# Layer norm of the next image in the selective scan's own PSUM pool, and the block's last copy in another place of ScalarE's queue

## The chip, the core and the metric

One core of one Trainium2 chip runs the whole program, a chain of four layers. The metric is the device time in microseconds, the median of several runs; less is better. One further execution was recorded by the hardware profiler, and all durations of single instructions come from it.

## The reference, cut to what matters

Two images of 128 channels and 64x64 pixels pass an attention layer, a convolution layer with deformed sampling, three steps of a residual convolution, and then the layer that is changed here, a selective scan in four directions:

```python
x_norm = _layernorm(x_flat, ln_w, ln_b)          # over the 128 channels of a pixel
def _mamba(x, ...):
    xh, z = jnp.split(x @ W_in.T, 2, axis=-1)
    xh = silu(causal_conv4(xh) + conv_b)
    dt, Bm, Cm = split(xh @ W_xp.T)
    dt = softplus(dt @ W_dt.T + b_dt)
    dA, dBu = exp(dt[..., None] * A), dt[..., None] * Bm[:, :, None, :] * xh[..., None]
    h_t = dA_t * h_{t-1} + dBu_t                 # 256 channels x 16 states, 4096 pixels
    y = einsum(h, Cm) + xh * Dp
    return (y * silu(z)) @ W_out.T
out = x + W_fuse @ concat(mamba of rows, rows reversed, columns, columns reversed) + b_fuse
```

## The kernel before, in words

The last layer is `layer3`. Each image and direction is cut into 8 **blocks** of 512 pixels, so there are 64 blocks, numbered i: image 0's four directions (rows; columns; columns reversed; rows reversed), then image 1's (columns; columns reversed; rows; rows reversed). A block has 8 **groups** k (two halves of 128 channels times four sets of four states), and each group four **scans** of 128 x 512 on VectorE. A group's place in its block, k mod 8, is called its slot. The order of all work is written by hand: within `tc.manual_schedule()` each engine's queue holds its instructions in the order in which the Python code issues them, and the framework adds the waits.

Four PSUM pools share the memory: `psd` (three tiles `da`, the decays), `psb` (two `pbc`), `psy` (one `py`) and `psm` (two `pm3`, for everything else).

One turn of the main loop, for group k in slot s of block i:

- `weights(k + 2)` on TensorE (L1370) spreads B over partitions into `pbc`.
- Four times: `expo` on ScalarE (L1402) makes the decay `da` of the scan that is two ahead; in the first of the four, `keep` (L1416) saves the last state of the group before; `scan` on VectorE (L1411). An expo needs a free `da`, so it waits for the scan that read that tile last. In two slots of a block `gate` (L1438) stands between the second and the third scan.
- `db_dve` (L1386, VectorE) and `db_pool` (L1395, GpSimd) make the inputs of the next group's scans, `cmul` (L1421, GpSimd) multiplies the scanned states by C.
- The front of the *next* block by slot: slot 0 `conv_silu` (ScalarE, L1289, L1290, with two loads of activation tables); 1 `xproj` and `xproj_copy`; 2 and 3 `delta` (TensorE, L1334) and `softplus` (ScalarE, four instructions, L1340 to L1343), one half each; 4 `xproj_rest` (L1326, L1327) and `rest_copy` (L1330); 5 `zproj` (L1296) and `zproj_silu` (L1302, L1303); 6 and 7 `conv` (L1284), one half each.
- The end of the *previous* block: in slot 3 `project` on TensorE (L1446 adds the old pixels by an identity matrix, L1448 twice the output weights) into a `pm3` tile; in slot 4, after everything else that ScalarE does there, `finish`, one copy out of that tile: L1454 in a first direction, L1456 in the second and third, L1459 in the last, to a tile named `sq` that is then stored.
- `sums(k - 2)` on TensorE (L1429) adds up a group over its states, which frees its `db` buffer, one of four.

Layer norm of image 0 runs ahead of the loop, in a prologue over `t`, in which the front of block 0 is spread too. Layer norm of image 1 is done during blocks 22 to 29, 512 pixels in each, by `next_norm`. Before the change its steps are: slot 6 `ln_mean` (TensorE, L1211, by a matrix of 1/128, into a `pm3` tile); slot 7 `ln_square` (VectorE subtracts the mean, L1222; ScalarE squares, L1223); and in the next block slot 0 `ln_var` (TensorE, L1227, another `pm3`); slot 1 `ln_scale` (ScalarE, L1231 Ln and L1232 Exp; GpSimd multiplies, L1233); slot 2 `ln_store` (ScalarE, L1242). It stands at the end of a turn, ahead of `sums`. Image 1's `sq` and `xc` are single buffers, and `sq` is shared with the result tile of L1459.

```python
                for q in range(4):
                    if 4 * k + q + AHEAD < len(units):
                        expo(*units[4 * k + q + AHEAD])
                    if q == 0 and ended:
                        keep(k - 1)
                    if live:
                        scan(k, q)
                ...
                front_pe(i + 1, slot)
                front_act(i + 1, slot)
                front_pool(i + 1, slot)
                if i >= 1 and i <= NBK:
                    if slot == 3:
                        project(i - 1)
                    elif slot == 4:
                        finish(i - 1)
```

Of the kernel before, what the change touches and what calls it, by code (L numbers as in the profile page):

```python
# [10 lines left out]
F32 = mybir.dt.float32  # L11
# [4 lines left out]
AF = mybir.ActivationFunctionType  # L16
# [4 lines left out]
P = 128  # L21
NB = 2
HW = 64
L = HW * HW
BLK = 512
NBLK = L // BLK
RB = BLK // HW
# [25 lines left out]
def interior(g, b, r0=0, rows=HW):  # L53
    return g.xa[:, b, 1 + r0 : 1 + r0 + rows, 1 : 1 + HW]
# [7 lines left out]
def img(t):  # L62
    return t.rearrange("p (r w) -> p r w", w=HW)
# [1057 lines left out]
def layer3(g, I, out):  # L1121
# [5 lines left out]
    nc, tc = g.nc, g.tc  # L1127
# [6 lines left out]
    with ExitStack() as ctx:  # L1134
# [71 lines left out]
        N = {}  # L1206


        def ln_mean(b, k):
            N[k, "mean"] = psm.tile([P, BLK], F32, name="pm3")  # L1210
            nc.tensor.matmul(N[k, "mean"], onesm, interior(g, b, k * RB, RB), start=True, stop=True)  # L1211

        def ln_square(b, k):
            if b == 0:

                t = wk.tile([P, 4, BLK], F32, name="db")
                N[k, "xc"], N[k, "sq"] = t[:, 0, :], t[:, 1, :]
            else:
                N[k, "xc"] = ck.tile([P, BLK], F32, name="xc", bufs=1)
                N[k, "sq"] = ck.tile([P, BLK], F32, name="sq", bufs=1)  # L1220
            xc = N[k, "xc"]
            nc.vector.tensor_sub(img(xc), interior(g, b, k * RB, RB), img(N[k, "mean"]))  # L1222
            nc.scalar.activation(N[k, "sq"], xc, AF.Square)  # L1223

        def ln_var(b, k):
            N[k, "var"] = psm.tile([P, BLK], F32, name="pm3")
            nc.tensor.matmul(N[k, "var"], onesm, N[k, "sq"], start=True, stop=True)  # L1227

        def ln_scale(b, k):

            nc.scalar.activation(N[k, "sq"], N[k, "var"], AF.Ln, bias=g.eps5)  # L1231
            nc.scalar.activation(N[k, "sq"], N[k, "sq"], AF.Exp, scale=-0.5)  # L1232
            nc.gpsimd.tensor_mul(N[k, "xc"], N[k, "xc"], N[k, "sq"])  # L1233

        def by_row(k):
# [214 lines left out]
        def finish(i):  # L1450
            b, nd, c = blocks[i]
            s_ = S.pop(i)
            if nd == 0:
                nc.scalar.activation(s_["xv"], img(s_["pf"]), AF.Identity, bias=vec(g, "b_fuse"))  # L1454
            elif nd < 3:
                nc.scalar.copy(s_["xv"], img(s_["pf"]))  # L1456
            else:
                res = ck.tile([P, BLK], F32, name="sq", bufs=1)
                nc.scalar.copy(res, s_["pf"])  # L1459
                nc.sync.dma_start(out[b, :, c * BLK : (c + 1) * BLK], res)  # L1460

# [62 lines left out]
                if slot in (3, 4):  # L1524
                    spread(i, slot - 3)

        LN = {6: ln_mean, 7: ln_square, 8: ln_var, 9: ln_scale, 10: ln_store}

        def next_norm(i, slot):

            for j, s in ((i, slot), (i - 1, slot + 8)):
                b, k = divmod(j, 4 * NBLK)
                k -= 4 * NBLK - 2 - NBLK
                if j >= 0 and b + 1 < NB and 0 <= k < NBLK and s in LN:
                    LN[s](b + 1, k)

        with tc.manual_schedule():
            tc.keep_in_program_order(nc.scalar.preload_act_table_set("natural_log_exp_and_others"))
            nc.scalar.activation(am, am, AF.Exp)
            nc.vector.tensor_scalar(am, am, -1.0, None, ALU.mult)  # L1540
            nc.vector.memset(xt[:, :HC], 0.0)
            nc.vector.memset(xt[:, HC + L :], 0.0)
            nc.vector.memset(xn[:, HB - 1, HW - HC :], 0.0)
            nc.vector.memset(xn[:, HB + HW, :HC], 0.0)

            for t in range(NBLK + 2):
                slot = t - 2
                if slot == 6:
                    for k in range(2):
                        weights(k)  # L1550
                    db_dve(0)
                    db_pool(0)
                if slot >= 0:
                    front_pe(0, slot)
                    front_act(0, slot)
                    front_pool(0, slot)
                if slot == 1:
                    bc_store(0)
                elif slot in (3, 4):
                    spread_store(0, slot - 3)  # L1560
                    if slot == 3:
                        spread_load(0, 0)
                        copies(0, "b", 0)
                        copies(0, "c", 0)
                for s in LN:
                    if 0 <= t - s // 8 < NBLK:
                        LN[s](0, t - s // 8)
                if t == 1:
                    begin(0)
                    conv(0, 1)  # L1570
            for ng in range(1, NNG):
                copies(0, "b", ng)
                copies(0, "c", ng)
            units = [(k, q) for k in range(len(groups)) for q in range(4)]
            AHEAD = 2
            for u in range(AHEAD):
                expo(*units[u])
            for k in range(len(groups) + 6):
                i, slot = divmod(k, 8)
                live = k < len(groups)  # L1580
                more = k + 1 < len(groups)
                ended = 1 <= k <= len(groups)
                transfers(i + 1, slot)
                if k + 2 < len(groups):
                    weights(k + 2)
                for q in range(4):
                    if 4 * k + q + AHEAD < len(units):
                        expo(*units[4 * k + q + AHEAD])
                    if q == 0 and ended:
                        keep(k - 1)  # L1590
                    if live:
                        scan(k, q)

                    for j, hf in (((k - 6) // 8, 0), ((k - 10) // 8, 1)):
                        if q == 1 and 8 * j + 6 + 4 * hf == k and 0 <= j < NBK:
                            gate(j, hf)
                if more:
                    db_dve(k + 1)
                    db_pool(k + 1)
                if ended:  # L1600
                    cmul(k - 1)
                front_pe(i + 1, slot)
                front_act(i + 1, slot)
                front_pool(i + 1, slot)
                if i >= 1 and i <= NBK:
                    if slot == 3:
                        project(i - 1)
                    elif slot == 4:
                        finish(i - 1)
                if live:  # L1610
                    next_norm(i, slot)

                    if slot == 6 and i % (4 * NBLK) < NBLK // 2:
                        for n in range(2):
                            turn(blocks[i][0], 2 * (i % (4 * NBLK)) + n)

                if 0 <= k - 2 < len(groups):
                    sums(k - 2)
# [159 lines left out]
```

## Time and profile before

| what | value |
|---|---|
| median of 3 runs | 5967.48 us (5966.78 to 5974.58) |
| the profiled execution: its own time | 5965.63 us |
| the profiled execution: span from first to last instruction | 5963.8 us |
| busy: TensorE, VectorE, ScalarE, GpSimd | 4905.1, 4521.3, 3768.4, 3653.1 us |
| first scan starts, last scan ends | 2517.65, 5948.17 us |
| granted TensorE clock, mean | 0.86 |

The span in 40 slices of 149 us; a digit is the busy share in tenths, PEclk the granted clock in tenths:

```profile
DVE  5333333364134688599999999999999999999998
ACT  4888888830035411477666766767776766767665
POOL 5111111100010121299999999999999999999998
PEclk8999999999989899877778777877788777877776
```

From slice 18 on it is the scan stage: VectorE and GpSimd are full, ScalarE is at two thirds, and TensorE's clock changes all the time. In the groups of instructions, a line gives the busy us, the mean ns of one, and the idle time of its engine just before, with what ended it. In a list of waits a line gives who waited, for whom, the us in total, how many times and the longest. A timeline line gives start, length, engine, line, operation, tiles (out<-in) and shape; equal neighbours are merged, and a bracket holds idle time before it and its releaser.

### The profile page before, as it was taken

To read this page: it belongs to the slowest core of one execution; us is meant where nothing else is said; L and a number is where in the kernel's file an instruction comes from. 1 tells how busy PE (TensorE), PEld (TensorE's weight loads), DVE (VectorE), ACT (ScalarE), POOL (GpSimd) and SP (SyncE) were. 2 spreads that over 40 slices of the span, in tenths; PEclk is the share of its full clock that TensorE was granted. 3 is DMA by queue.
4 is the path that set the end of the run, shared out by engine and by line. 5 is a ranking of instruction groups with operands and counts; after the bars stand their busy time and mean duration, and the time that the engine had idled before them with its cause. 6 is when DMAs were issued, how large, how long until landed. Compare 5 with 4: busy or idle time off the path is not lost.

```text
span 5963.8 us, 57478 instructions
## 1 busy us (share of the span) xinstructions
PE 4905.1 (82%) x18726; PEld 1661.7 (28%) x18726; DVE 4521.3 (76%) x4266; ACT 3768.4 (63%) x5371; POOL 3653.1 (61%) x1328
## 2 busy tenths in 40 slices
PE   7999999989978689877777777777777777777776
PEld 3333333334444234222222222222222222222221
DVE  5333333364134688599999999999999999999998
ACT  4888888830035411477666766767776766767665
POOL 5111111100010121299999999999999999999998
PEclk8999999999989899877778777877788777877776
DMA  5000001030066100255555555554565555555554
GB/s 153 18 18 18 19 18 33 1 58 1 15 116 113 48 4 0 52 135 123 125 126 139 135 123 124 128 134 116 136 139 131 127 122 130 139 130 126 126 136 99
DMA packets 333092, 541.85 MB, mean 91 GB/s; under 512 B 66504, under 2 KB 121168, under 8 KB 331696
## 3 DMA queue, kind: packets, MB, share of 16 engines
q1 hardware_dynamic: 329648, 534.54, 39.0%
q10 hardware_dynamic: 3136, 3.56, 0.2%
q8 instruction: 149, 2.44, 0.2%
q14 instruction: 159, 1.30, 0.1%
HBM read 448.78 MB, written 89.13 MB: 90 GB/s over the span
## 4 chain that ended last, share of the span: by engine, by line
PE 39%; DVE 37%; ACT 6%; issue 6%; DMA 6%; POOL 4%; SPq 1%; DVEq 0%; POOLq 0%; ACTq 0%
DVE db L1411 25%; PE ps L287 10%; DVE db L1386 10%; PE acc L303 8%; PE m L1052 5%; PE m L566 5%; DMA dx<-dd 3%; POOL db L1421 2%; ACT da L1402 2%; PE acd L812 2%; PE pm L1296 1%; PE m L526 1%; ACT L1303 1%; ACT L1302 1%; PE pf L775 1%
## 5 line engine op out<-in xcount | busy, mean ns | idle before, releaser
L1421 POOL TENSOR_TENSOR db<-db,c 128x2048 f32<-128x2048 f32 x512 | 2310.7, 4528 | 21.6 <-ACT hl L1416 21.1
L1411 DVE TENSOR_TENSOR_SCAN db<-da,hl,db 128x512 f32<-128x512 f32 x1792 | 2165.0, 1265 | 61.3 <-ACT da L1402 14.9
L1402 ACT ACTIVATE da<-dd,am 128x512 f32<-128x512 f32 x2048 | 1403.5, 689 | 963.3 <-DVE db L1411 953.7
L293 ACT ACTIVATE e<-ps 128x1024 f16<-128x1024 f32 x1024 | 992.2, 1021 | 134.7 <-PE ps L287 117.5
L1386 DVE TENSOR_TENSOR db<-pbc,dd 128x2048 f32<-128x2048 f32 (+2 forms) x512 | 851.8, 1664 | 19.8 <-PE py L1429 18.2
L1370 PE MATMUL pbc<-bc,sel 64*128 64x512 f32 x512 | 288.5, 564 | 571.7 <-DVE db L1386 571.4
L1395 POOL TENSOR_TENSOR db<-b,dd 128x1024 f32<-128x1024 f32 (+1 forms) x256 | 671.6, 2623 | 119.9 <-issue 94.5
L1429 PE MATMUL py<-db,fold 128*32 128x512 f32 x4096 | 640.5, 703 | 104.8 <-POOL db L1421 104.7
L314 DVE RECIPROCAL rec<-acc 32x512 f32<-32x512 f32 x64 | 214.9, 3358 | 639.2 <-PE acc L303 612.1
L321 POOL TENSOR_TENSOR parts<-parts 32x512 f32<-32x512 f32 x64 | 80.4, 1256 | 975.3 <-DVE parts L320 975.3
L287 PE MATMUL ps<-q,k 32*128 32x512 f32 x4096 | 656.2, 643 | 3.5 <-DVE flag L250 2.7
L303 PE MATMUL acc<-e,v 128*128 128x512 f16 x2048 | 531.3, 382 | 0.0
L1052 PE MATMUL m<-v,u 128*128 128x512 f32 x864 | 377.2, 600 | 51.0 <-DVE v L1021 51.0
L1370 PEld LDWEIGHTS pbc<-bc,sel 64*128 64x128 f32 x512 | 106.2, 208 | 1113.4 <-DVE db L1386 1048.3
L1284 PE MATMUL pm<-xn,wcs 128*128 128x512 f32 x512 | 285.0, 708 | 56.9 <-DVE xc L1222 46.3
L1411 DVE TENSOR_TENSOR_SCAN db<-da,db 128x512 f32<-128x512 f32 x256 | 294.4, 1205 | 17.4 <-ACT da L1402 8.7
L303 PEld LDWEIGHTS <-v 128*128 128x128 bf16 x2048 | 158.5, 97 | 509.8 <-issue 388.5
L287 PEld LDWEIGHTS ps<-q,k 32*128 32x128 f32 x4096 | 229.7, 183 | 227.9 <-issue 147.1
L1284 PE MATMUL pm<-xt,wcs 128*128 128x512 f32 x512 | 279.2, 696 | 11.3 <-ACT z L1302 11.3
L1427 PE MATMUL py<-u,ddp 128*128 128x512 f32 x256 | 186.4, 818 | 101.7 <-DVE gt L1438 101.7
L566 PE MATMUL m<-comb,w 64*128 64x512 f32 (+4 forms) x1296 | 269.9, 575 | 0.0
L686 POOL TENSOR_SCALAR yt<-y 32x512 f32<-32x512 f32 x8 | 18.2, 2270 | 381.2 <-DVE y L677 380.8
(315 smaller groups left out, 5970.5 us busy)
## 6 DMA issues: line engine op xcount, KB each, us to landing
dd<-dx SPq DMA_DIRECT2D x1024, 256.0 KB, 6.6
dx<-dd SPq DMA_DIRECT2D x128, 512.0 KB, 8.7
c<-bx SPq DMA_DIRECT2D x1024, 64.0 KB, 2.3
hats<-pos SPq DMA_DIRECT2D x136, 256.0 KB, 9.6
b<-bx SPq DMA_DIRECT2D x512, 64.0 KB, 5.2
q<-qd SPq DMA_DIRECT2D x32, 512.0 KB, 8.6
w<-in_conv0T SPq DMA_DIRECT2D x18, 288.0 KB, 8.5
q<-in_x SPq DMA_DIRECT2D x8, 512.0 KB, 7.6
```

The lines of the kernel that those rows point to most:

```text
L287: nc.tensor.matmul(ps[:, i, :], k4[h % 2][rows, kb // 4, :], q4[h % 2][rows, qb * BLK : (qb + 1) * BLK], start=True, stop=True,)
L293: nc.scalar.activation(e[:, :n, :], ps[:, :n, :], AF.Exp)
L303: nc.tensor.matmul(acc, v3[b][:, kb, h, :], e[:, i, :], start=(kb == 0), stop=(kb == NS - 1))
L566: yield lambda q=q, dy=dy, src=src, i0=i0, i1=i1: nc.tensor.matmul(m[:, i0 * NF : i1 * NF], w[half, dy, q, x, :], src, start=(dy == KC and ...
L1052: nc.tensor.matmul(m[x], weights[j][:, dy, x, :], v[j][b][:, x, r0 : r0 + RP, :].rearrange("p r i -> p (r i)"), start=(dy == 0), stop=(dy ...
L1284: nc.tensor.matmul(pu, wcs[:, hf, s, :], window(blk, sgn * s), start=(s == 0), stop=(s == 3))
L1386: nc.vector.tensor_tensor(x["db"][:, :n, :], x.pop("pb").unsqueeze(1).to_broadcast([P, n, BLK]), S[i]["d4", hf][:, 1, :n, :], ALU.mult)
L1395: nc.gpsimd.tensor_tensor(x["db"][:, n:, :], S[i]["b", ng].unsqueeze(1).to_broadcast([P, 4 - n, BLK]), S[i]["d4", hf][:, 1, n:, :], ALU.mult)
L1402: nc.scalar.activation(da, S[i]["d4", hf][:, 0, q, :], AF.Exp, scale=am[:, hf, q, ng : ng + 1])
L1411: nc.vector.tensor_tensor_scan(d1, d0, d1, 0.0 if first else hl[:, hf, ng, q, :], ALU.mult, ALU.add)
L1421: nc.gpsimd.tensor_mul(v, v, S[i]["c", ng].unsqueeze(1).to_broadcast([P, 4, BLK]))
L1429: nc.tensor.matmul(S[i]["y", hf][32 * q : 32 * q + 32, :], fold, G[k]["db"][:, q, :], start=False, stop=(ng == NNG - 1),)
```

## The change

It has four parts, all in `layer3`.

1. Mean and variance of layer norm are written to `da` tiles of `psd` instead of `pm3` tiles of `psm`, in the prologue and in the loop.
2. In the loop, the steps of image 1's layer norm stand in other slots, in the turn of the same block: slot 0 `ln_mean` (right after the first expo) and `ln_less` (the subtraction, after the scans); slot 1 `ln_square` (now the square alone, after `xproj_copy`); slot 3 `ln_var` (after the first expo), `ln_log` (before the last expo) and `ln_root` (after softplus); slot 4 `ln_scale` (GpSimd's multiplication alone); slot 6 `ln_store`. In the prologue their order stays.
3. `finish` is issued at the start of slot 4, ahead of the four expos, for every block.
4. The result tile of L1459 gets a name and so a buffer of its own; the loop has one more turn.

```diff
+        def ln_tile():
+            return psd.tile([P, BLK], F32, name="da")
+
         def ln_mean(b, k):
-            N[k, "mean"] = psm.tile([P, BLK], F32, name="pm3")
+            N[k, "mean"] = ln_tile()
             nc.tensor.matmul(N[k, "mean"], onesm, interior(g, b, k * RB, RB), start=True, stop=True)
 
-        def ln_square(b, k):
+        def ln_less(b, k):
...
-            xc = N[k, "xc"]
-            nc.vector.tensor_sub(img(xc), interior(g, b, k * RB, RB), img(N[k, "mean"]))
-            nc.scalar.activation(N[k, "sq"], xc, AF.Square)
+            nc.vector.tensor_sub(img(N[k, "xc"]), interior(g, b, k * RB, RB), img(N[k, "mean"]))
+
+        def ln_square(b, k):
+            nc.scalar.activation(N[k, "sq"], N[k, "xc"], AF.Square)
 
         def ln_var(b, k):
-            N[k, "var"] = psm.tile([P, BLK], F32, name="pm3")
+            N[k, "var"] = ln_tile()
             nc.tensor.matmul(N[k, "var"], onesm, N[k, "sq"], start=True, stop=True)
 
+        def ln_log(b, k):
+            nc.scalar.activation(N[k, "sq"], N[k, "var"], AF.Ln, bias=g.eps5)
+
+        def ln_root(b, k):
+            nc.scalar.activation(N[k, "sq"], N[k, "sq"], AF.Exp, scale=-0.5)
+
         def ln_scale(b, k):
-            nc.scalar.activation(N[k, "sq"], N[k, "var"], AF.Ln, bias=g.eps5)
-            nc.scalar.activation(N[k, "sq"], N[k, "sq"], AF.Exp, scale=-0.5)
             nc.gpsimd.tensor_mul(N[k, "xc"], N[k, "xc"], N[k, "sq"])
...
-                res = ck.tile([P, BLK], F32, name="sq", bufs=1)
+                res = ck.tile([P, BLK], F32, name="res", bufs=1)
...
-        LN = {6: ln_mean, 7: ln_square, 8: ln_var, 9: ln_scale, 10: ln_store}
-
-        def next_norm(i, slot):
-            for j, s in ((i, slot), (i - 1, slot + 8)):
-                b, k = divmod(j, 4 * NBLK)
-                k -= 4 * NBLK - 2 - NBLK
-                if j >= 0 and b + 1 < NB and 0 <= k < NBLK and s in LN:
-                    LN[s](b + 1, k)
+        def next_norm(i):
+            b, k = divmod(i, 4 * NBLK)
+            k -= 4 * NBLK - 2 - NBLK
+            return (b + 1, k) if b + 1 < NB and 0 <= k < NBLK else None
...
-                for s in LN:
-                    if 0 <= t - s // 8 < NBLK:
-                        LN[s](0, t - s // 8)
+                if t < NBLK:
+                    for part in (ln_mean, ln_less, ln_square):
+                        part(0, t)
+                if 0 <= t - 1 < NBLK:
+                    for part in (ln_var, ln_log, ln_root, ln_scale, ln_store):
+                        part(0, t - 1)
...
-            for k in range(len(groups) + 6):
+            for k in range(len(groups) + 7):
...
+                norm = next_norm(i)
+                if slot == 4 and 1 <= i <= NBK:
+                    finish(i - 1)
                 for q in range(4):
+                    if norm and slot == 3 and q == 3:
+                        ln_log(*norm)
                     if 4 * k + q + AHEAD < len(units):
                         expo(*units[4 * k + q + AHEAD])
+                    if norm and q == 0:
+                        if slot == 0:
+                            ln_mean(*norm)
+                        elif slot == 3:
+                            ln_var(*norm)
                     if q == 0 and ended:
                         keep(k - 1)
...
+                if norm and slot == 0:
+                    ln_less(*norm)
                 if more:
                     db_dve(k + 1)
                     db_pool(k + 1)
...
-                if i >= 1 and i <= NBK:
-                    if slot == 3:
-                        project(i - 1)
+                if slot == 3 and 1 <= i <= NBK:
+                    project(i - 1)
+                if norm:
+                    if slot == 1:
+                        ln_square(*norm)
+                    elif slot == 3:
+                        ln_root(*norm)
                     elif slot == 4:
-                        finish(i - 1)
+                        ln_scale(*norm)
+                    elif slot == 6:
+                        ln_store(*norm)
                 if live:
-                    next_norm(i, slot)
```

## The prediction, made before the run

> **What bounds the kernel now.** I read the page's costliest groups first. The scan stage (2517.6 to 5948.2 us in the trace, 58% of the span) belongs to VectorE; it waits 61 us in all before 1792 scans, and most of ScalarE's idle time is waiting for scans.
>
> ```profile
> L1411 DVE TENSOR_TENSOR_SCAN db<-da,hl,db 128x512 f32<-128x512 f32 x1792 | 2165.0, 1265 | 61.3 <-ACT da L1402 14.9
> L1402 ACT ACTIVATE da<-dd,am 128x512 f32<-128x512 f32 x2048 | 1403.5, 689 | 963.3 <-DVE db L1411 953.7
> ```
>
> Then busy time by stretch (columns: busy us of PE, PEld, DVE, ACT, POOL with counts, clock, DMA): before the blocks that also normalise image 1 (22 to 29), during them, after them.
>
> ```profile
> 2517.60:3688.50 1170.90, 886.02 (x2510) 246.41 (x2509) 1146.38 (x924) 822.04 (x1330) 1120.44 (x351) 0.80 0.56 130
> 3688.50:4190.70 502.20, 382.76 (x1068) 112.09 (x1068) 474.48 (x386) 353.79 (x572) 471.27 (x153) 0.79 0.54 127
> 4190.70:5948.20 1757.50, 1321.15 (x3752) 366.02 (x3752) 1720.39 (x1385) 1212.01 (x1965) 1687.82 (x524) 0.79 0.55 129
> ```
>
> VectorE is 98% busy outside and 94% inside the middle stretch. From first scan to first scan a block takes 53.49 us (51.73 for the last of a direction, since scans without an initial state are shorter); the nine blocks 22 to 30 take 502.3 instead of 9 x 53.49 - 1.75 + 8 x 0.60 = 484.5 us, where 0.60 is what the added subtraction takes of VectorE's queue. So about **17.8 us** can be won there. The waits of 3742 to 4191 us say where they lie:
>
> ```profile
> DVE db L1386 <- PE py L1429: 18.2, 8, 2.9
> PE pm L1284 <- DVE xc L1222: 46.3, 8, 6.2
> ```
>
> The mean sits in a `pm3` tile (two buffers) until VectorE's L1222, so conv's second half (L1284) waits for it on TensorE, the sums (L1429) queue behind it, and L1386 misses its db buffer.
>
> Next ScalarE from slot 3 to slot 5 of block 19 (start, us): the end of softplus, the expo that the third scan of slot 4 reads, the two copies. Then TensorE and VectorE there.
>
> ```profile
> 3554.89 0.72 ACT L1343 ACTIVATE dd<-dd,cst 128x512 f32<-128x512 f32 x1
> 3555.51 0.67 ACT L1402 ACTIVATE da<-dd,am 128x512 f32<-128x512 f32 x1
> ...
> 3560.42 0.57 ACT L1330 CAST bc<-pm 32x512 fp32r<-32x512 f32 x1 [1.24 <-PE pm L1327]
> 3561.02 1.14 ACT L1456 COPY xa<-pm 128x512 f32<-128x512 f32 x1
> ```
> ```profile
> 3549.47 2.07 PE L1334 MATMUL pm<-xd,wdt 8*128 8x512 f32 x2
> 3551.47 2.27 PE L1446 MATMUL pm<-xa,ident 128*128 128x512 f32 x2
> 3553.55 3.23 PE L1448 MATMUL pm<-gt,mt 128*128 128x512 f32 x4
> ```
> ```profile
> 3548.80 4.81 DVE L1411 TENSOR_TENSOR_SCAN db<-da,hl,db 128x512 f32<-128x512 f32 x4
> 3553.52 1.20 DVE L1386 TENSOR_TENSOR db<-pbc,dd 128x1024 f32<-128x1024 f32 x1
> 3554.82 4.81 DVE L1411 TENSOR_TENSOR_SCAN db<-da,hl,db 128x512 f32<-128x512 f32 x4
> ```
>
> Call the start of slot 3's first scan T (3548.80). Softplus ends at T+6.81, the project at T+7.98, the expo at T+7.38, and its scan, third of the second four at 1.18 us each, starts at T+8.40: **about 1 us of slack**, for one ScalarE queue. In block 20 (T = 3602.28) the same project ends at T+6.16:
>
> ```profile
> 3605.69 2.76 PE L1448 MATMUL pm<-gt,mt 128*128 128x512 f32 x4
> ```
>
> Over the blocks this end takes three values in turn, about 6.0 to 6.5, 7.4 to 7.7, and 7.9 to 8.35. The clock is the reason: two windows of block 19, the first and the last of four of 3.4 us.
>
> ```profile
> 3548.80:3552.20 3.40, 3.40 (x4) 1.22 (x5) 3.40 (x3) 1.80 (x4) 3.40 (x2) 0.50 0.00 0
> 3559.00:3562.40 3.40, 2.91 (x14) 0.67 (x13) 3.30 (x3) 2.14 (x4) 3.40 (x2) 1.00 0.42 149
> ```
>
> **The skill.** (1) "TensorE: Matmul & The Clock Gate", Part 1: the gate gives half or full clock and is decided in free-running windows of 3413 ns. The trace agrees: 0.50 and 1.00 above. (2) "PSUM — Partial Sum Buffer", Engine vs sequencer instructions: ScalarE's queue is strict FIFO. It agrees: all its instructions stand in program order, L1330's wait holds up L1456. (3) "ScalarE: Activation LUTs", What ACT_TABLE_LOAD costs: consecutive ACTIVATEs overlap by about 93 ns; here 0.72 us from 3554.89 ends at 3555.61, the next starts at 3555.51.
>
> **Part 1: finish goes ahead of slot 4's expos (all 64 blocks).** Nothing is added; the copy of 0.58 to 1.28 us is moved past four expos, keep and rest_copy. There it starts behind softplus *and* waits for the project, with the expos queued behind it, and VectorE behind those. The data for the third scan is then ready at max(6.81, P) + F - 0.09 + 0.69 + 0.04, with P the project's end, F finish's length, 0.69 the expo and 0.04 the lag from L1327's end (3560.38) to L1330's start. The stall is that less 8.40: max(6.81, P) + F - 7.76, never below 0. F by the trace: L1454 0.69 (image 0), 1.25 (image 1); L1456 1.16 for columns, 0.59 for rows; L1459 0.58. So a row costs 0 at early P and 0.9 to 1.2 at late P; a column 0.2 and 1.3 to 1.8. Summed with each block's own P, the 55 blocks outside 22 to 29 lose 37 us.
>
> But P depends on T's place in the clock's window: read over 63 blocks, 6.0 to 6.5 for places 0.7 to 1.7 us, then a jump to 8.35 that falls by 0.47 per us of later T to 7.4. A block takes 53.49 = 15.67 windows, hence three values in turn. A stall of 1.12 us makes it 16 windows: the next block meets the same place; one that comes later finds a smaller P, one that comes earlier a greater. So the stall settles near 1.1 us, after a few blocks of each direction. Carried from block to block by these numbers, 55 blocks lose **50 us** (48 to 51 whatever the first place). Early release of the project's PSUM tile gains 0: nobody waits for it except zproj, 7 times, 1.7 us in all.
>
> **Part 2: layer norm in the loop (blocks 22 to 29).** The 17.8 us above go: mean and variance leave `pm3`, so conv no longer waits. Instead they take a third of the `da` buffers. In slot 0, mean waits for the first scan, and each later expo for a scan later than before; the fourth starts at 4.82 instead of 3.65, then conv_silu (3.86 us) and the next expo end at 10.09, when its scan is due at 10.05: 0.1 to 0.2 us, 8 times, 1.2. The subtraction itself is in both. In slot 3 the variance matmul waits on TensorE for the first scan (T+1.3) ahead of delta and project, and takes 1.0 to 2.0 us. On ScalarE the fourth expo starts at T+4.85 instead of 3.67, softplus then runs to 7.9 and ln_root (0.63) to 8.54; so finish can't start before that. The stall is max(8.54, P + 2.0) + F - 7.76: at least 1.35 for a row, 1.95 for a column. Below, no credit is possible, since FIFO holds; above, P of 8.35 + 2 gives 3.2 to 3.8. With the places carried on it sums to 20.5 (range 13 to 27). Net: 20.5 + 1.2 - 17.8 = **+4**. The rest moves beside other work: Square behind xproj_copy, where the following expo ended 3 us before its scan; POOL's multiply (1.26 us) from slot 1 of the next block to slot 4, within a 53 us block in which POOL works 52; ln_store (1.28) behind slot 6's expos, where ScalarE then idles 2.8.
>
> **Part 3: prologue.** Order is unchanged; only PSUM differs. The last mean waited 3.6 us for z's tile and the last Ln 1.7 us for TensorE, which had conv ahead of the variance; the first scan waits 7.6 us for ScalarE, which is behind that norm. With tiles of their own I follow ScalarE's queue to a first scan some 3 us earlier; 0 to 5 are the bounds. POOL and the loads then come last. The `res` tile and the one more turn of the loop issue nothing new: **-3**, together.
>
> **Sum** against the profiled execution, 5965.6 us (span 5963.8): +50 + 4 - 3 = 6017. The median shown is 1.9 above, so I say **6018**.
>
> **Rivals.** (A, forecast, 65%) as above; 6007 to 6028. (B, 18%) The stall doesn't settle, because the stalled blocks change TensorE's busy windows and P stays spread: 37 + 4 - 3 = 38, so 6005; with Part 2's stall at its lower end (13 for 20.5) and the prologue at -5, 5996. (C, 10%) Slot 3 is worse: variance and project fall wholly into half clock and rest_copy too is late: 8 x 4 more, 6040. (D, other side, 7%) Project ends before softplus nearly always, that is at or below T+6.81, because matmuls are earlier or faster than the modelled ends: then rows cost 0, columns 0.2 x 31 = 6, slot 3's wait is hidden too, and 17.8 + 3 are won: 5968 - 15 = 5953. It decides from P = 7.2 for a row. Against it: L1330 started 0.04 us after L1327's modelled end each time it waited. That the change doesn't do what it says is excluded by the order of instructions, in which finish precedes the expo.
>
> **Numbers.** A measurement here tells 0.2% (12 us) from no change. Faster takes half of D, same the rest of D and a corner of B: faster 0.04, same 0.04, slower 0.92. Range 5996 to 6031: A, B with its unknowns at their low ends, and the near part of C.
>
> **What would show it.** Right: idle time before scans, released by the expo, some 1.1 us in slot 4 of nearly every block, and a block of about 54.6 us; finish waiting for project on ScalarE; L1386's waits for sums gone in blocks 22 to 30; blocks 22 to 29 at 55.5 to 57.5. Wrong: blocks still at 53.49 outside them, project ending by T+6.8, or a prologue that moved by more than 5 us.

## The result, and the profile after

| what | before | after |
|---|---|---|
| median of 4 runs | 5968.15 us (5966.78 to 5974.58) | 6036.87 us (6034.98 to 6040.17) |
| profiled execution: own time, span | 5965.63, 5963.8 | 6037.43, 6035.6 |
| first scan starts, last scan ends | 2517.65, 5948.17 | 2513.39, 6019.97 |
| length of blocks 0 to 21, us | 1170.8 | 1196.1 |
| length of blocks 22 to 30, us | 502.3 | 518.0 |
| length of blocks 31 to 63, us | 1757.4 | 1792.5 |

After over before is **1.0114**, 95% interval 1.0096 to 1.0131. The direction was as forecast; the time is 19 us above 6018, and 6 us above the range. Lines after the change: scan L1420 (was L1411), expo L1411, keep L1425, db_dve L1395, db_pool L1404, cmul L1430, sums L1438, weights L1379, delta L1343, softplus L1349 to L1352, rest_copy L1339, project L1455 and L1457, finish L1463, L1465, L1468; norm's variance L1232, log L1236, root L1239.

The two groups, as shown of before:

```profile
L1420 DVE TENSOR_TENSOR_SCAN db<-da,hl,db 128x512 f32<-128x512 f32 x1792 | 2173.0, 1267 | 134.2 <-ACT hl L1425 67.5
L1411 ACT ACTIVATE da<-dd,am 128x512 f32<-128x512 f32 x2048 | 1398.5, 689 | 1017.9 <-DVE db L1420 1006.9
```

The work is the same to 0.4%. What grew is VectorE's idle time before scans, from 61.3 to 134.2 us. The releaser named is keep, L1425; it stands right behind the first expo of slot 4, so the name doesn't tell which of the two the scan waited for, but both stand behind finish. Busy time by stretch, same columns as before:

```profile
2513.40:3709.50 1196.10, 908.40 (x2508) 255.60 (x2508) 1148.86 (x924) 821.44 (x1329) 1122.61 (x351) 0.78 0.55 127
3709.50:4227.50 518.00, 407.95 (x1063) 112.90 (x1067) 476.49 (x386) 351.80 (x572) 471.99 (x153) 0.77 0.52 123
4227.50:6020.00 1792.50, 1356.16 (x3760) 378.31 (x3752) 1724.16 (x1385) 1211.28 (x1965) 1688.88 (x524) 0.77 0.54 126
```

VectorE's and ScalarE's busy us are those of before within 4 us in each row; only the lengths differ. Now block 19 again (T = 3566.21): ScalarE, then TensorE, then VectorE.

```profile
3572.30 0.72 ACT L1352 ACTIVATE dd<-dd,cst 128x512 f32<-128x512 f32 x1
3574.11 1.13 ACT L1465 COPY xa<-pm 128x512 f32<-128x512 f32 x1 [1.08 <-PE pm L1457]
3575.01 0.71 ACT L1411 ACTIVATE da<-dd,am 128x512 f32<-128x512 f32 x1
```
```profile
3566.88 2.07 PE L1343 MATMUL pm<-xd,wdt 8*128 8x512 f32 x2
3568.88 2.26 PE L1455 MATMUL pm<-xa,ident 128*128 128x512 f32 x2
3570.96 3.11 PE L1457 MATMUL pm<-gt,mt 128*128 128x512 f32 x4
```
```profile
3572.24 2.46 DVE L1420 TENSOR_TENSOR_SCAN db<-da,hl,db 128x512 f32<-128x512 f32 x2
3575.82 2.46 DVE L1420 TENSOR_TENSOR_SCAN db<-da,hl,db 128x512 f32<-128x512 f32 x2 [1.13 <-ACT hl L1425]
```

Read it from left to right: softplus ends at T+6.81, as before; finish waits 1.08 us for the project (its end P is T+7.86); the expo ends at T+9.51; the third scan of slot 4 stands idle 1.13 us. The prediction's formula gives 7.86 + 1.13 - 7.76 = 1.23. The scan starts at T+9.61 in place of T+8.40, 1.21 us late: 1.13 of idle time, and 0.08 by which a scan otherwise starts before the one ahead of it has ended. TensorE's clock there (a window, its length, TensorE's busy us and count, the granted clock, DMA share, GB/s):

```profile
3572.20:3573.20 1.00, 1.00 (x2) 0.50 0.00 0
3573.20:3574.20 1.00, 1.00 (x6) 0.88 0.00 0
```

0.88 over 1 us means 0.24 us at half and the rest at full: the clock rises at 3573.44, T+7.23, and the project ends 0.63 us later.

Now block 26, one of those that normalise image 1 (T = 3962.16): TensorE, ScalarE, VectorE, clock.

```profile
3963.49 2.08 PE L1232 MATMUL da<-sq,onesm 128*128 128x512 f32 x2 [0.59 <-DVE db L1420]
3965.50 2.07 PE L1343 MATMUL pm<-xd,wdt 8*128 8x512 f32 x2
3967.50 2.08 PE L1455 MATMUL pm<-xa,ident 128*128 128x512 f32 x2
3969.37 3.59 PE L1457 MATMUL pm<-gt,mt 128*128 128x512 f32 x4
```
```profile
3970.06 0.61 ACT L1239 ACTIVATE sq<-sq 128x512 f32<-128x512 f32 x1
3973.00 0.58 ACT L1468 COPY res<-pm 128x512 f32<-128x512 f32 x1 [2.32 <-PE pm L1457]
```
```profile
3974.28 2.46 DVE L1420 TENSOR_TENSOR_SCAN db<-da,hl,db 128x512 f32<-128x512 f32 x2 [3.64 <-ACT hl L1425]
```
```profile
3971.00:3972.00 1.00, 1.00 (x3) 0.50 0.09 37
3972.00:3973.00 1.00, 1.00 (x6) 0.60 1.01 410
3973.00:3974.00 1.00, 1.00 (x9) 1.00 0.20 78
```

The variance (2.08 us at half clock) comes first; the project ends at T+10.81. The clock rises at 3972.80, T+10.64, which is 3.41 us after the place in block 19. In both blocks it had gone to half at T-6.42, and it stays there for 13.65 us in block 19 and 17.07 in block 26: four windows, and five. The place of T in the window is the same, so the blocks can be compared in this. VectorE waits 3.64 us for it (10.81 + 0.58 - 7.76 = 3.63). The waits of VectorE in 3709.5 to 4227.5:

```profile
DVE db L1420 <- ACT hl L1425: 30.2, 9, 4.6
DVE db L1420 <- POOL db L1404: 3.2, 8, 0.8
```

The 18.2 us in which db_dve waited for the sums (L1386 for L1429 before) no longer occur.

For comparison, delta and project of a row block without the variance, block 51 (T = 5336.91), in which P is T+8.16:

```profile
5337.59 2.07 PE L1343 MATMUL pm<-xd,wdt 8*128 8x512 f32 x2
5341.45 3.62 PE L1457 MATMUL pm<-gt,mt 128*128 128x512 f32 x4
```

Delta starts at T+0.68 here and at T+3.34 in block 26. The variance moves it by 2.66 us: it takes 2.0, and it starts 0.66 later than delta would, since it waits for the first scan.

Steady blocks outside 22 to 29 take 54.60 us, and the last ones inside (25 to 28) 58.03 to 58.08. That is 16 and 17 times 3.413 us. In columns the lengths come down to it by halves: blocks 17 to 21 take 55.13, 54.87, 54.74, 54.68, 54.64. That is the slope of P in the prediction: from block 17 to 18 T comes 0.51 us later in the window and P falls by half as much, from 8.24 to 7.99. In rows P stays at 8.16, its value with the clock at half all through, and nothing halves (blocks 1 to 3 take 54.69 each); so whether the rows too are held, experiments 5 and 12 have to show.

### The profile page after: what moved, and what is told of

Same layout as the page of the kernel before. It is cut to its first block, busy times and chain, and to the rows that moved or that the text cites. A ratio compares the mean times of both kernels' runs of the same rounds, so it can differ in the third digit from the quotient of the medians.

```text
span 6035.6 us, 57411 instructions
## 1 busy us (share of the span) xinstructions
PE 4986.5 (83%) x18726; PEld 1684.3 (28%) x18726; DVE 4529.1 (75%) x4266; ACT 3764.8 (62%) x5371; POOL 3655.7 (61%) x1328
## 4 chain that ended last, share of the span: by engine, by line
PE 44%; DVE 37%; ACT 8%; issue 5%; POOL 3%; DMA 2%; SPq 1%; DVEq 0%; POOLq 0%; ACTq 0%
DVE db L1420 24%; DVE db L1395 10%; PE ps L287 10%; PE acc L303 8%; PE m L1052 5%; PE m L566 4%; PE pm L1457 3%; ACT da L1411 2%; PE pm L1455 2%; PE pm L1343 2%; PE acd L812 2%; POOL db L1430 1%; PE m L526 1%; ACT L1312 1%; ACT L1311 1%
## 5 line engine op out<-in xcount | busy, mean ns | idle before, releaser
L1430 POOL TENSOR_TENSOR db<-db,c 128x2048 f32<-128x2048 f32 x512 | 2310.3, 4528 | 103.0 <-ACT hl L1425 100.8
L1420 DVE TENSOR_TENSOR_SCAN db<-da,hl,db 128x512 f32<-128x512 f32 x1792 | 2173.0, 1267 | 134.2 <-ACT hl L1425 67.5
L1411 ACT ACTIVATE da<-dd,am 128x512 f32<-128x512 f32 x2048 | 1398.5, 689 | 1017.9 <-DVE db L1420 1006.9
L1395 DVE TENSOR_TENSOR db<-pbc,dd 128x2048 f32<-128x2048 f32 (+2 forms) x512 | 853.4, 1667 | 7.3 <-DMA dd<-dx 7.3
L1379 PE MATMUL pbc<-bc,sel 64*128 64x512 f32 x512 | 291.7, 570 | 603.1 <-DVE db L1395 602.9
L1404 POOL TENSOR_TENSOR db<-b,dd 128x1024 f32<-128x1024 f32 (+1 forms) x256 | 671.8, 2624 | 112.1 <-issue 99.9
L1438 PE MATMUL py<-db,fold 128*32 128x512 f32 x4096 | 619.9, 681 | 100.1 <-POOL db L1430 100.1
L1379 PEld LDWEIGHTS pbc<-bc,sel 64*128 64x128 f32 x512 | 107.0, 209 | 1124.9 <-DVE db L1395 1030.7
L1420 DVE TENSOR_TENSOR_SCAN db<-da,db 128x512 f32<-128x512 f32 x256 | 294.9, 1206 | 27.7 <-ACT hl L1425 12.3
L686 POOL TENSOR_SCALAR yt<-y 32x512 f32<-32x512 f32 x8 | 18.2, 2271 | 382.0 <-DVE y L677 381.6
```

What stands on the lines that cost most here:

```text
L1395: nc.vector.tensor_tensor(x["db"][:, :n, :], x.pop("pb").unsqueeze(1).to_broadcast([P, n, BLK]), S[i]["d4", hf][:, 1, :n, :], ALU.mult)
L1404: nc.gpsimd.tensor_tensor(x["db"][:, n:, :], S[i]["b", ng].unsqueeze(1).to_broadcast([P, 4 - n, BLK]), S[i]["d4", hf][:, 1, n:, :], ALU.mult)
L1411: nc.scalar.activation(da, S[i]["d4", hf][:, 0, q, :], AF.Exp, scale=am[:, hf, q, ng : ng + 1])
L1420: nc.vector.tensor_tensor_scan(d1, d0, d1, 0.0 if first else hl[:, hf, ng, q, :], ALU.mult, ALU.add)
L1430: nc.gpsimd.tensor_mul(v, v, S[i]["c", ng].unsqueeze(1).to_broadcast([P, 4, BLK]))
L1438: nc.tensor.matmul(S[i]["y", hf][32 * q : 32 * q + 32, :], fold, G[k]["db"][:, q, :], start=False, stop=(ng == NNG - 1),)
```

## The experiments

In a block's account below, "wait in slot 4" is the idle time of VectorE before slot 4's scans, read from the trace; 0.10 us of it stands ahead of the first of them in every block. The start of layer 3, and the first scan with it, moved by up to 5.5 us from kernel to kernel (first mean at 2447.7 to 2457.2, before at 2453.2), also where the code ahead of it is equal; so I compare lengths of the scan stage too: 3430.5 us before, 3506.6 after.

**1 and 2: finish alone.** First the changed kernel with finish put back:

```diff
-                if slot == 4 and 1 <= i <= NBK:
-                    finish(i - 1)
...
+                    elif slot == 4:
+                        finish(i - 1)
```

> The changed kernel with finish back at the end of slot 4; layer norm's tiles and slots stay as changed. Theory (finish ahead of the expos is the whole loss outside blocks 22 to 29): those blocks return to 53.49 us, which gives back 61 us; blocks 22 to 29 keep a stall of 0.8 to 0.9 us in slot 4, because ln_root now stands between softplus and the expo, and 0.3 us at the multiplication: about 54.1 + 1.2 each. Prologue 4 us shorter than before. Sum 5968 - 4 - 18 + 9 = 5955. Rival (moving layer norm and its da tiles cost a good part, by making TensorE late): blocks 22 to 29 stay above 57 us and the time above 5975.

Measured 5954.85 us (5949.93 to 5957.57), ratio to before 0.9975 (0.9967 to 0.9984). Outside 22 to 29 the blocks are back at 53.50; the scan stage takes 3424.6.

Then the kernel before with finish moved to the start of slot 4, and nothing else:

> The kernel before with one edit, finish at the start of slot 4. Theory: a stall of 1.1 us in nearly every block, whatever layer norm does, so 61 us outside blocks 22 to 29, and some 9 us more inside them on top of what they lose before: 6038. Rival (the lost time comes from finish and layer norm together, for instance by TensorE's clock): less than 40 us over the kernel before, 6008 or less.

Measured 6030.41 us (6028.21 to 6031.48), ratio 1.0102 (1.0085 to 1.0119), 8 below what I expected. Blocks 0 to 21 take 1195.6 us and 31 to 63 1791.9, as in the changed kernel. Blocks 22 to 30 take 508.4, 6.1 more than before: where db_dve waits for sums as of old, the block comes to another place in the clock's window, and in four of the eight the project ends before T+6.4 and VectorE waits 0.1 us at most for it. Finish alone costs 62 us, the rest alone gains 13.5; their sum is 48.5, and the change costs 69. Some 20 us arise only where both meet. 16.5 of them lie in blocks 22 to 30 (518.0 us with both; 508.4 and 495.4 with one of the two; 502.3 with neither).

**3: which part of finish's place.** The changed kernel with finish ahead of slot 4's third expo in place of the first:

```diff
-                if slot == 4 and 1 <= i <= NBK:
-                    finish(i - 1)
                 for q in range(4):
+                    if slot == 4 and q == 2 and 1 <= i <= NBK:
+                        finish(i - 1)
```

> The changed kernel with finish two expos later in slot 4, before the third. Theory (what counts is which expo is queued behind the copy): the two expos that slot 4's own scans need are ahead of it, the next one is not needed for 3 us, so no stall outside blocks 22 to 29, although finish still waits for the project on ScalarE; time as with finish at the end of the slot, 5955. Rival (any wait of ScalarE for the project in this slot costs what it lasts): a stall of 0.5 to 1 us remains per block, 5990 to 6015.

Measured 5952.76 us (5951.51 to 5957.48), ratio 0.9974 (0.9965 to 0.9983).

```profile
L1420 DVE TENSOR_TENSOR_SCAN db<-da,hl,db 128x512 f32<-128x512 f32 x1792 | 2167.5, 1266 | 67.3 <-ACT da L1411 17.5
```

The copy is as long as before, but two expos are out ahead of it, and that is enough: blocks are at 53.50, in 22 to 29 at 54.0 to 55.7. Outside these finish now waits for the project in 8 blocks only, 0.3 us each, so the wait is tried in 22 to 29 alone: there slot 4's third scan stands idle for 0.71 us in block 28, where finish waits 1.06, and for 0.72 in blocks 26 and 27, where it doesn't wait. So neither the copy nor its wait costs anything in slot 4 where the two expos that are due stand ahead of them.

**4: the project earlier.** The changed kernel with `project` in slot 2.

```diff
-                if slot == 3 and 1 <= i <= NBK:
+                if slot == 2 and 1 <= i <= NBK:
                     project(i - 1)
```

> The changed kernel with project a slot earlier (slot 2, right after the gate that it needs); finish stays ahead of slot 4's expos. Theory (the stall is the wait for the project, made long by TensorE's half clock; the copy itself nearly fits): rows 53.49, columns 53.7 to 53.8, blocks 22 to 29 bounded by softplus and ln_root, 55.5 to 56.3. Sum 5968 - 4 + 8 - 18 + 16 = 5970. Rival (the copy's own length is the loss, its wait hides behind softplus): rows lose 0.6 and columns 1.2 us still, 6010 to 6025.

Measured 5995.20 us (5993.30 to 5997.14), ratio 1.0046 (1.0029 to 1.0062): 25 above what I expected. The wait for finish is gone: slot 4's waits outside 22 to 29 sum to 6.8 us, where the changed kernel has 60.8 and the kernel before 5.8. Rows are at 53.50. Columns are at 54.60, by a wait in slot 6 for db_pool. The project and the db_pool behind it, of a row (block 5) and of a column (block 13):

```profile
2791.29 1.13 PE L1455 MATMUL pm<-xa,ident 128*128 128x512 f32 x2
2792.26 1.88 PE L1457 MATMUL pm<-gt,mt 128*128 128x512 f32 x4
...
2796.16 2.36 POOL L1404 TENSOR_TENSOR db<-b,dd 128x1024 f32<-128x1024 f32 x1 [1.27 <-issue]
```
```profile
3222.42 2.16 PE L1455 MATMUL pm<-xa,ident 128*128 128x512 f32 x2
3224.40 3.51 PE L1457 MATMUL pm<-gt,mt 128*128 128x512 f32 x4
...
3229.93 2.36 POOL L1404 TENSOR_TENSOR db<-b,dd 128x1024 f32<-128x1024 f32 x1 [3.22 <-issue]
```

In the column the project runs at half clock, 2.6 us longer; the sums behind it, which free a db buffer, end at 3229.76, and db_pool starts 0.17 us later. GpSimd waits 2 us longer than in the row and works without a pause from there to slot 6, so it is late at the scan. The project moved, and took the clock's wait to another engine, with the same block length.

**5: a longer copy.** In the rows, finish does its copy twice:

```diff
+            turns = 1 if dirs[b][nd][1] else 2
...
+                for _ in range(turns):
-                nc.scalar.copy(s_["xv"], img(s_["pf"]))
+                    nc.scalar.copy(s_["xv"], img(s_["pf"]))
```

> The changed kernel with the finish copy done twice in the row directions, so that 0.59 us more of ScalarE stands ahead of slot 4's expos in each row block. Theory (the block locks to whole windows of 3.413 us: a longer copy only lets the block meet an earlier project end, and the sum stays): row blocks stay at 54.6 us with a stall of 1.0 to 1.1 us, the project's end falls from T+8.16 to about T+7.6, and the whole stays at 6037, within 4 us. Rival (the stall is the sum of project end, copy and expo, with the project's end fixed): 31 row blocks at 0.59 us more, 6037 + 18 = 6055.

Measured 6050.05 us (6048.43 to 6051.13), ratio 1.0140 (1.0123 to 1.0157): 13 above the theory's number and 5 below the rival's, so neither was met. Both are seen in the blocks (us; P is the project's end after T):

```
block                       49     50     51     52     53     54     55
changed kernel, length   54.59  54.59  54.60  54.60  54.60  54.60  54.60
changed kernel, P         8.14   8.16   8.16   8.16   8.16   8.16   8.16
copied twice, length     55.22  54.91  54.77  54.68  54.65  54.63  54.62
copied twice, P           8.15   7.85   7.70   7.62   7.59   7.57   7.56
```

The first row block of a direction pays the copy in full; then P falls by as much as the copy is longer (8.16 to 7.56), and the block is at 54.6 again. So the block is held, but the way there costs: 11.8 us of scan stage in all (3518.4), and blocks 9, 33 and 56, which had no wait in the changed kernel, have one.

**6: da tiles alone.** The kernel before, with only the mean and the variance in da tiles:

```diff
-            N[k, "mean"] = psm.tile([P, BLK], F32, name="pm3")
+            N[k, "mean"] = psd.tile([P, BLK], F32, name="da")
...
-            N[k, "var"] = psm.tile([P, BLK], F32, name="pm3")
+            N[k, "var"] = psd.tile([P, BLK], F32, name="da")
```

> The kernel before with only this of the change: mean and variance are written to da tiles; norm's steps and finish keep their old places. Theory (what the change was worth is the wait of conv for the mean's tile, and the prologue): blocks 22 to 30 lose their 17.8 us but for what the da buffers cost, the first scan is 3 to 4 us earlier, so 5968.4 - 18 - 4 = 5947, at most 5950. Rival (a third of the da buffers costs about as much as it gives, 0.7 us of waiting for an expo and 0.4 for GpSimd in each of eight blocks, as with the new places): 5955.

Measured **5945.28 us** (5941.84 to 5949.95), ratio 0.9966 (0.9953 to 0.9978): the fastest of all. Blocks 22 to 30 take 487.0 us; the wait of db_dve for sums is gone, and what is left there is GpSimd's (VectorE's waits of 3680 to 4170 us):

```profile
DVE db L1411 <- POOL db L1395: 6.2, 8, 2.0
```

The scan stage is 14.2 us shorter than before; 2.4 us lie between the first mean and the first scan (62.06 for 64.42), and 5.5 in an earlier start of layer 3, which I can't explain by the edit. With norm's new slots as well, and finish at its old place (experiment 1), blocks 22 to 30 take 495.4: the new slots cost 8.4 us against da tiles in the old ones.

**7 and 8: the variance out of slot 3.** The changed kernel with variance, log and root in slot 2:

```diff
-                    if norm and slot == 3 and q == 3:
+                    if norm and slot == 2 and q == 3:
                         ln_log(*norm)
...
-                        elif slot == 3:
+                        elif slot == 2:
                             ln_var(*norm)
...
-                    elif slot == 3:
+                    elif slot == 2:
                         ln_root(*norm)
```

> The changed kernel with variance, log and root of the norm in slot 2 in place of slot 3, finish as in the changed kernel. Theory (blocks 22 to 29 pay for the variance ahead of the project on TensorE, which puts its end at T+10.8): without it they are like the others, 54.6 to 55.2 us instead of 58.05, 8 x 3.1 = 25 less: 6012, 6008 to 6018. Rival (the eight blocks pay for the da buffers that norm takes, in whatever slot): 58 us in them, 6037.

Measured 6017.61 us (6017.31 to 6019.22), ratio 1.0086 (1.0069 to 1.0103). Blocks 22 to 30 fall from 518.0 to 498.2. VectorE's waits there (3709 to 4208 us):

```profile
DVE db L1420 <- POOL db L1404: 12.0, 8, 2.6
DVE db L1420 <- ACT hl L1425: 2.2, 1, 2.2
```

Of the 30.2 us 28 are gone, so the place of these three steps made them. That it is the variance on TensorE, not log and root on ScalarE, is read in the changed kernel's trace: finish stands ready and waits 1.2 to 2.6 us for the project in each of blocks 22 to 29. But 9 come back as GpSimd's: in block 26 the variance and delta at half clock put the sums' end 3.6 us behind what db_pool wanted, as in experiment 4.

The same move with finish ahead of the third expo:

> The same move of variance, log and root to slot 2, with finish ahead of the third expo of slot 4 (two expos later than in the changed kernel). Theory: nothing is left that makes slot 4's scans wait; blocks 22 to 29 fall from 55.3 to about 54.1 us (53.5 and the subtraction's 0.6), so 5952.8 - 8 x 1.1 = 5944, 5941 to 5950. Rival (da buffers cost the same in slot 2): 5953.

Measured 5961.03 us (5954.73 to 5967.25), ratio 0.9988 (0.9981 to 0.9994); the expectation was missed by 17. 6 us are the first scan (2518.1), with a later start of layer 3. Blocks 22 to 30 take 497.2 us, 2.4 more than in experiment 3: the waits of 0.7 us in slot 4 are gone, and waits of 1.1 to 3.1 us for db_pool are there instead. Slot 2 is no better place for norm than slot 3.

**9, 10, 11: work added to VectorE, first try.** If a stalled block is held to whole windows, 0.60 us more on VectorE should vanish in its wait. After slot 0's scans of every block:

```diff
+                if live and slot == 0:
+                    for _ in range(1):
+                        nc.vector.tensor_sub(spare, spare, spare)
```

In the changed kernel:

> The changed kernel with one more subtraction on VectorE (128x512, 0.60 us, of a tile that nothing else reads) after the scans of slot 0 of every block. Theory (a block whose wait ends on the project is held to 16 windows of 3.413 us = 54.60 us): work that VectorE adds is taken out of the wait; the wait in slot 4 falls from 1.0 to about 0.4 to 0.5 us, blocks stay at 54.6 and blocks 22 to 29 at 58.03, the whole stays at 6037, at most 6043. Rival (the wait is a fixed sum of durations, and 54.60 is an accident): 64 x 0.60 = 38 more, 6075.

The same twice:

> The same with two subtractions, 1.20 us in each block. 53.50 + 1.20 = 54.70 is just over 16 windows. Theory: the wait in slot 4 nearly vanishes in most blocks, a block takes about 54.7 to 54.8 us, and the whole is 55 x 0.1 to 0.25 above the changed kernel, 6042 to 6055. Rival (fixed sum): 64 x 1.20 = 77 more, 6114.

And in experiment 1's kernel, as a control:

> The control: the changed kernel with finish back at the end of slot 4 (5954.9 us), and one subtraction more in each block. Here no scan waits for the project, so both theories expect the subtraction to be paid in full: 64 x 0.60 = 38 more, 5993. If it comes out under 5975, VectorE's queue isn't what bounds a block, and the run of the changed kernel with one more says nothing on windows.

Measured 6188.14 us (6179.98 to 6194.11), 6342.57 (6342.11 to 6349.85) and, the control, 6127.84 (6118.94 to 6133.30): ratios 1.0374 (1.0357 to 1.0391), 1.0629 (1.0611 to 1.0647) and 1.0270 (1.0253 to 1.0287). All miss by far, the control too, so they tell nothing on windows. VectorE and GpSimd of the control:

```profile
2851.12 2.11 DVE L1619 TENSOR_TENSOR spare<-spare 128x512 f32<-128x512 f32 x1
```
```profile
2843.67 9.00 POOL L1430 TENSOR_TENSOR db<-db,c 128x2048 f32<-128x2048 f32 x2
2852.63 2.81 POOL L1404 TENSOR_TENSOR db<-b,dd 128x1024 f32<-128x1024 f32 x1
```
```profile
L1619 DVE TENSOR_TENSOR spare<-spare x64: 666/2760/5082, 2518.3 to 6058.5; 128x512 f32<-128x512 f32 x64
```

The last line has the shortest, median and longest ns. The subtraction took 0.67 us in the one block where GpSimd was idle; in nearly all others it stood until GpSimd's instruction ended (here at 2852.67) and 0.56 us longer. The Trainium skill says so ("SBUF — State Buffer", SBUF: two separate sides): a VectorE operation with two SBUF inputs and a GpSimd operation that reads SBUF lock each other out for a whole instruction. The trace agrees for VectorE's side, at 2.7 us on average; I had not thought of it, since norm's own subtraction has one input in PSUM and took 0.66.

**12, 13, 14: the same with one input in PSUM.** The subtraction reads slot 0's last da tile, behind its scan:

```diff
+            if k % 8 == 0 and q == 3:
+                for _ in range(1):
+                    nc.vector.tensor_sub(spare, d0, spare)
```

> The changed kernel with one more subtraction on VectorE in each block, after the last scan of slot 0, and with one of its two inputs in PSUM (the da tile of that scan), as norm's own subtraction has it, which took 0.66 us and moved its followers by 0.60. Theory (a block whose wait ends on the project is held to 16 windows of 3.413 us): the wait in slot 4 falls from 1.0 to about 0.4 to 0.5 us, blocks stay at 54.6 and blocks 22 to 29 near 58.03; the whole 6037, at most 6045. Rival (the wait is a fixed sum of durations): 64 x 0.60 = 38 more, 6075.

Measured 6047.80 us (6045.67 to 6051.43), ratio 1.0138 (1.0121 to 1.0155): 11 above the changed kernel, not 38, and 3 above the most that I had allowed. VectorE in slot 4 of block 51, the third scan of the changed kernel and then this one:

```profile
5346.39 2.46 DVE L1420 TENSOR_TENSOR_SCAN db<-da,hl,db 128x512 f32<-128x512 f32 x2 [0.99 <-ACT hl L1425]
```
```profile
5350.93 2.46 DVE L1420 TENSOR_TENSOR_SCAN db<-da,hl,db 128x512 f32<-128x512 f32 x2
5353.81 2.46 DVE L1420 TENSOR_TENSOR_SCAN db<-da,hl,db 128x512 f32<-128x512 f32 x2 [0.42 <-ACT hl L1428]
```

The wait fell from 0.99 to 0.42, by what was added, and blocks 50 to 55 are at 54.61 to 54.63. Columns don't settle: they alternate, 54.13 without a wait and 55.0 with 0.8 to 0.9, which is 54.6 on average. Blocks 22 to 30 take 518.4. The 11 us lie where a direction begins, above all in blocks 9, 33 and 56, as in experiment 5.

The control, with finish at the end:

> The control: the changed kernel with finish back at the end of slot 4 (5954.9 us), and the same subtraction with a PSUM input. Both theories expect it to be paid in full, 64 x 0.60 = 38 more: 5993. Under 5980 VectorE's queue isn't what bounds a block and the run before it says nothing on windows; much over 6000 it waits for GpSimd, as the subtraction of two SBUF inputs did.

Measured 5992.32 us (5989.29 to 5999.75), ratio 1.0043 (1.0026 to 1.0060): paid in full, 40 us of scan stage, 54.09 per block.

Two subtractions:

> The changed kernel with two such subtractions in each block, 1.20 us: 53.50 + 1.20 = 54.70 is just over 16 windows. Theory: the wait in slot 4 nearly vanishes in most blocks, a block takes 54.7 to 54.9 us, the whole is 55 x 0.1 to 0.3 above the changed kernel, 6042 to 6055. Rival (fixed sum): 77 more, 6114.

Measured 6085.20 us (6078.89 to 6091.08), ratio 1.0204 (1.0187 to 1.0221), 48 above the changed kernel; neither theory's number. The block without a wait takes 54.82, which is 1.32 more than 53.50 where I had counted 1.20, and 0.22 beyond 16 windows. Rows run four blocks or more without a wait, until the place has drifted to where P is 8.16; then two blocks wait. Columns run two at most, then wait (P 8.35, then 7.5; 56.55 and 55.7 us). So the hold ends where the block is longer than its 16 windows by itself; after that the place drifts and the wait comes now and then.

## Why the prediction was right in direction and 19 us short

Against the profiled executions, before 5965.63 and after 6037.43, the sum is:

| step | predicted | measured |
|---|---|---|
| part 1, finish ahead of the expos, 55 blocks | +50 | +61.1 (25.3, block 30's 0.85, 35.0) |
| part 2, norm in the loop, blocks 22 to 29 and what they leave in 30 | +4 | +14.9 |
| part 3, prologue | -3 | -4.3 |
| sum | +51 | +71.8 |

Part 1's mechanism, place and block length were right: the stall in slot 4, behind finish, behind the project; about 1 us of wait; 54.6 us per block. Experiments 1 and 3 show that it is the order of finish and expos, 5 and 12 that the hold is real (a longer copy, or more VectorE work in rows, comes out of the wait once a direction has settled). That the clock's window does the holding is read from the lengths, 16 and 17 windows, and from experiment 14, where the hold ends past the 16th; the window itself was not varied. Short was its sum, by 11: the carry gave 0.9 us per block on average, while 51 of the 55 blocks wait, and cost 1.1 to 1.2. I counted more blocks with an early project after a change of direction than there are (9, 33 and 56, and the last), and took the deadline T+8.40 for the first block of a direction, whose scans are shorter and are due earlier: blocks 8, 16, 32, 40 and 48 wait 1.35 to 1.74 us. A stall costs also 0.1 us more than its idle time (54.61 with 1.00 in block 13): scans that follow one another overlap by 0.08, a scan that has waited doesn't, and the one behind it is another 0.03 late. And by its own formula a row at a late P (7.9 to 8.35) costs 0.7 to 1.2, not 0.9 to 1.2; in the trace of before a row's P ends at 8.16, and 8.35 is a column's.

**Two terms of the sum were too small, by 11 us each: part 1's carry, 50 where 61.1 was measured, as just told, and part 2's "max(8.54, P + 2.0) + F - 7.76", 20.5 where 29.4 was measured (30.2 with 0.7 in block 30).** With one of them right, the time would have been some 6029, within 5996 to 6031. The second lay beyond its own range of 13 to 27, and its step was wrong, not only its size. "P + 2.0" took P from a block without the variance and added the variance's duration. It left out that the variance starts later than delta would, 0.66 us by the lines above, though the same paragraph says that it waits for the first scan until T+1.3. And it left the clock alone: at the same place in the window TensorE stays at half clock for one window more (blocks 19 and 26). So P moves by more than 2 us at every place.

In experiment 3's kernel, where no block is held, the project of row blocks 25 to 29 ends at 10.4, 9.6, 9.6, 10.8 and 10.7 us after T; row blocks of the kernel before, at the same places, have 7.3, 6.0, 6.0, 8.2 and 7.6. That is 2.7 to 3.6 more. In the changed kernel P settles at T+10.8, 2.65 above a settled row's 8.16, and the block at 17 windows. Experiment 7 shows norm's place in slot 3 as the cause (28 of the 30 us go with it). How much of the longer stay at half clock comes from the wait of 0.66 us and how much from the 2 us of work was not tried. Besides, 3.2 us of waits for db_pool were not in the sum, and the 1.2 us that it has for slot 0 did not come; 29.4 + 3.2 - 17.8 is the 14.9 measured, to 0.1.

The rest of part 2 held: the 17.8 us of conv and sums went. Experiment 6 takes that gain alone and keeps most of it (15.2 of 17.8). My rival C came close to the cause: it said "wholly into half clock", and I gave it 10%. That it came close to the time is luck: 8 x 4 more on 6018 is 6050, not 6040, and in place of the 20.5 it is 6030. Rival B (no settling) is refuted by the block lengths, rival D by finish's waits. In part 3 the size is right: from the first mean to the first scan it is 60.80 us for 64.42, 3.6 less. The other 0.6 is an earlier start of layer 3, which moves by more than that from kernel to kernel.

## What to carry to other kernels

An instruction that waits for another engine belongs behind those that the bounding engine needs next, on an in-order queue; two expos further down made 84 us of difference here. Where such a wait ends on TensorE's work and the clock of that work comes in windows, the loop's length can be held to whole windows (54.60 and 58.03 us here), as long as the loop is shorter than that without the wait. Then an added matmul can cost more than its own duration (2.7 to 3.6 us for 2.0 here), and a small amount of work added elsewhere vanishes in part (of 38 us on VectorE 11 were paid). And take a change apart: here one of its four parts alone gained 14 us of scan stage, another cost 62.

## What the runs showed of the hardware that was not expected

- A loop whose wait ends on TensorE settled at 54.60 and 58.03 us, 16 and 17 windows of 3.413 us, within seven blocks or fewer, in columns with the excess halving each time. It held for copies of 0.59 and 1.13 us and for two of 0.59, with one more subtraction in the rows, and for a wait of GpSimd's in place of ScalarE's (experiment 4). With a subtraction more in columns the blocks alternated, 54.1 and 55.0 us, around the same mean. Past the 16 windows (54.82) it did not hold.
- The same subtraction of 128x512 on VectorE took 0.66 us with one input in PSUM and 2.7 us on average (0.67 to 5.1) with both in SBUF, beside a GpSimd that is nearly always busy (96% of blocks 0 to 21 before): 64 of them cost 37 us in one form and 173 in the other.
